# Reordering the first two steps of a windowed-attention and dynamic-convolution kernel on Trainium2

## The chip, the cores and the metric

The kernel runs on one core of one Trainium2 chip. The metric is the device time of one execution in microseconds (us), read as the median of several runs. TensorE is called PE below, its weight loads PEld, VectorE DVE, ScalarE ACT, GpSimd POOL and SyncE SP.

## The reference, cut to what matters

The input is 16 images of 192 channels and 56 x 56 pixels in float32. Layer 0 is a Swin block with shifted 7 x 7 windows and six heads of 32 channels; layer 1 is a depthwise 3 x 3 convolution whose taps are computed from the pooled image.

```python
# layer 0
h = layer_norm(x over channels, norm1_g, norm1_b)      # then roll by (-3, -3), cut into 64 windows of 49
q, k, v = split(win @ qkv_w + qkv_b);  q = q * 32 ** -0.5
attn = softmax(q @ k.T + rel_bias[REL_IDX] + mask)     # mask: 0 or -inf at the rolled edges
x1 = x + unroll((attn @ v) @ proj_w + proj_b)
y = gelu(layer_norm(x1, norm2_g, norm2_b) @ fc1_w + fc1_b) @ fc2_w + fc2_b
x = x1 + y
# layer 1
t = relu(batch_norm(x.mean(height, width) @ w1.T))
taps = (t @ w2.T + b2) * causal_mask                   # 4 of 9 taps survive
out = depthwise_conv3x3(x, taps) + bias
...
```

## The kernel before

An image is done in four steps (`STEPS`) of 784 pixels, sixteen windows each; a step's tokens are two halves of 392 columns. The steps are software-pipelined: while PE does the MLP of one step, the other engines do the softmax and the norms of others. A steady loop over the steps is preceded by a hand-written prologue, which loads and folds the parameters and takes steps 0, 1 and 2 far enough that the loop can start. Its first work on PE is the first layer of the MLP of step 0 (`ph`).

PSUM is used as four pairs of banks. `banks(name, k)` hands out pair `k`; a tile in a pair waits until all readers of the previous tile in that pair are done. So the numbers in the calls decide waits.

```python
def banks(name, k):
    return psum.tile([128, 2, 512], F32, tag=f"pair{k}", name=name)
...
def columns(rows, n, name, k):              # parameter rows to columns: copy, 2 transposes, copy
    nc.vector.tensor_copy(rows[:, DIM:256], rows[:, C0:DIM])
    pt = banks(f"{name}_p", k)[:, 0]
    ...
    nc.vector.tensor_copy(cols.rearrange("p c n -> p (c n)"), pt[:, 0 : 2 * n])
...
def fold_means(dst, n, name, k):            # ones @ weights: fq_m for qkv, ff_m for fc1
...
def shift(dst, raw, lo, n, be):             # one-column products: a norm's bias through a weight
    mm(dst, raw[:, 0, lo : lo + n], be[0], True, False)
    mm(dst, raw[0:64, 1, lo : lo + n], be[1][0:64], False, True)
...
def attention_scores(i, q4, q2, ks):        # sc on PE for 4 pairs of windows; bias added on DVE
    ...
    def top(wp):                            # DVE: max, subtract; ACT: exp
    def share(wp):                          # DVE: sum, reciprocal; POOL: prob = e / sum
```

The prologue's order is the order of recording, and each engine works off its own part of it in that order. Cut to what the argument touches, it runs so:

```python
# --- start
g1, be1, bq, bk, bv = columns(*rows1, 2)
...                                          # statistics of half 0 (st_a)
pm = fold_means(wqkv, 3 * DIM, "fq", 0)
fold_center(wqkv, 3 * DIM, pm)
nc.vector.memset(kbd, 0.0)
g2, be2, f2b, pb, cb = columns(*rows3, 1)
...                                          # 24 one-column products, qkb_p
norm_squares("1_1", 1, 0, nc.scalar, nc.vector)
norm1_scale(0, dvs.pop(0), nc.vector)
...                                          # biases of q and k; statistics st_b
...                                          # 14 loads rel_r and mask_t on SP
dvs.update(norm_spread(keys, dev, tags=("dv1", "yn0"), order=(0, 1)))
...                                          # parameter loads on POOL
# --- step 0
qs[0], outs = attention_qk(0, 1, 0, 3)
pvs, v_rest, v_whole = attention_v(0, (2, 1))
v_rest(); v_whole()
pv = banks("pb_p", 3)                        # 36 one-column products: folded biases of proj and fc1
...
table(AF.Exp)
for f in outs: f()                           # ACT: q and k out of PSUM
for t in vbd: nc.vector.memset(t, 0.0)
...                                          # 24 tiles bias_t on DVE
fold_scale(rawf, g2, wf1, ((0, 0, HID, 1.0),))
...                                          # three adds of pb_p on DVE
attention_v_out(pvs)                         # v out of PSUM, DVE and ACT
top, share = attention_scores(0, *qs.pop(0), (3, 0, 2, 1))
...                                          # transposes of w1 (w1p)
pm = fold_means(wf1, HID, "ff", 0)           # ff_m
qs[1], outs = attention_qk(1, 2, 3, 1)
...                                          # softmax of step 0
prts = [attention_turn(0, wp, (2, 0)[wp % 2]) for wp in range(4)]     # pt
# --- steps 1 and 2
pos = attention_values(0, prts, 1, 2)                                  # po
o = attention_rows(0, pos)
pvs, v_rest, v_whole = attention_v(1, (0, 3)); v_rest(); v_whole()     # pv
...
pp, pair1, p_narrow, p_rest, p_whole = project(0, o, 1, 2)             # pp
p_narrow(); p_rest(); p_whole()
residual(0, pp, pair1)
norm_squares("2_0", 0, 1, nc.scalar)
top, share = attention_scores(1, *qs.pop(1), (0, 3, 2, 1))             # scores of step 1
qs[2], outs = attention_qk(2, 0, 3, 2, between)                        # statistics st_c inside
...                                          # softmax of step 1, square roots, table loads
prts = [attention_turn(1, wp, (0, 2)[wp % 2]) for wp in range(4)]
...
pos = attention_values(1, prts, 3, 0)
...                                          # v of step 2, projection of step 1
pairs = [0, 3, 1, 2]
for i in range(2, NS + 2):                   # the steady loop, first ph
    ...
```

Of the kernel before, what the change touches and what calls it, by code (L numbers as in the profile page):

```python
# [9 lines left out]
AF = mybir.ActivationFunctionType  # L10
ALU = mybir.AluOpType
# [25 lines left out]
def tile_swin_then_dynamic_conv(  # L37
# [102 lines left out]
    def columns(rows, n, name, k):  # L140
# [9 lines left out]
        nc.vector.tensor_copy(cols.rearrange("p c n -> p (c n)"), pt[:, 0 : 2 * n])  # L150
# [97 lines left out]
    def norm_squares(key, i, side, engine, adder=None, tags=None):  # L248
# [12 lines left out]
        for h in range(2):  # L261
            p = slice(h * 64, h * 64 + 64)
            (adder or nc.gpsimd).tensor_tensor(s0[p, h], s0[p, h], s1[p], ALU.add)  # L263
        sqs[key] = s0

# [559 lines left out]


    g1, be1, bq, bk, bv = columns(*rows1, 2)
# [17 lines left out]
    norm_root(part)  # L845
    nc.vector.reciprocal(part, part)
    norm_squares("1_2", 2, 1, nc.gpsimd)
    dvs.update(norm_spread(keys, dev, (nc.sync, nc.scalar)))
    pm = fold_means(wqkv, 3 * DIM, "fq", 0)
    fold_center(wqkv, 3 * DIM, pm)  # L850
    nc.vector.memset(kbd, 0.0)
    g2, be2, f2b, pb, cb = columns(*rows3, 1)
# [11 lines left out]
    norm_squares("1_1", 1, 0, nc.scalar, nc.vector)  # L864
    norm1_scale(0, dvs.pop(0), nc.vector)
# [4 lines left out]
    nc.vector.tensor_scalar(kb, pick, qkb[:, 1:2], None, ALU.mult)  # L870

# [5 lines left out]
    norm_root(part)  # L877
    nc.vector.reciprocal(part, part)


    side = 2 * WS - 1
    for j in range(2):
        for yq in range(WS):
            q = j * 64 + yq * WS
            nc.sync.dma_start(
                rel_r[q : q + WS].rearrange("p (y x) h -> p y (x h)", y=WS),
                bass.AP(
                    rel_bias.tensor,
                    yq * side * HEADS,
                    [[HEADS, WS], [side * HEADS, WS], [1, WS * HEADS]],  # L890
                ),
            )
    nc.sync.dma_start(mask_t, win_mask)
    dvs.update(norm_spread(keys, dev, tags=("dv1", "yn0"), order=(0, 1)))
    images[1] = load_x(1, nc.sync)
    norm_squares("1_3", 3, 0, nc.gpsimd)
    for t in prob:
        nc.gpsimd.memset(t, 0.0)
# [4 lines left out]
    for k, v in enumerate((running_var, running_mean, gamma, beta)):  # L903
        nc.gpsimd.dma_start(bn[:, k], v.rearrange("(o r) -> o r", o=1).broadcast_to([128, RED]))
    w2v = w2.rearrange("(c t) r -> c t r", t=9)[:, 0:NTAP, :]
# [8 lines left out]
    qs[0], outs = attention_qk(0, 1, 0, 3)  # L914
    pvs, v_rest, v_whole = attention_v(0, (2, 1))
    v_rest()
    v_whole()

    pv = banks("pb_p", 3)
# [8 lines left out]
    table(AF.Exp)  # L928
    for f in outs:
        f()  # L930
    for t in vbd:
        nc.vector.memset(t, 0.0)
    rel_hk = rel_r[:, ::-1, :].rearrange("p k h -> p h k")
    for r in range(2):
        for e in range(2):
            for half in range(2):
                for g in range(3):
                    h = 2 * half if g < 2 else 4
                    row_b = g == 1 or (g == 2 and half == 1)
                    cut = mask_t[:, int(r and row_b), e, :].rearrange("p (o k) -> p o k", o=1)  # L940
                    nc.vector.tensor_tensor(
                        bias_t[:, r, e, half].rearrange("p (h k) -> p h k", k=N)[
                            :, 2 * g : 2 * g + 2
                        ],
                        rel_hk[:, h : h + 2],
                        cut.broadcast_to([PW, 2, N]),
                        ALU.add,
                    )
    fold_scale(rawf, g2, wf1, ((0, 0, HID, 1.0),))
    for c in range(2):  # L950
        nc.vector.tensor_tensor(pb[c], pb[c], pv[:, 0, c : c + 1], ALU.add)
# [303 lines left out]
```

## Time and profile before

| | before |
|---|---|
| time, first three runs | 3168.89 us median (3168.42 to 3170.85) |
| span of the profiled execution, clock granted to PE | 3168.7 us, 0.991 |
| from the start to the first `ph` | 125.14 us |
| from the first `ph` to the end of the span | 3043.6 us |
| PE idle before the first `ph` | 26.7 us |

The prediction below shows the main lines of this profile. One more cut of it carries the later argument. The next fence is PE's timeline of the kernel before; its columns are the start, the length, the engine, the line, the operation and its tiles, the count, and in brackets the idle time before it with what ended it.

```profile
94.25 1.48 PE L92 MATMUL pe<-win,wqkv 128*128 128x392 f32 x4
99.84 0.86 PE L519 MATMUL pt<-ident,prob 113*128 113x113 f32 x6 [4.11 <-ACT q L397]
103.56 3.63 PE L519 MATMUL pt<-ident,prob 113*128 113x113 f32 x18 [2.86 <-POOL prob L506]
111.47 5.37 PE L92 MATMUL po<-prt,vbd 128*64 128x49 f32 x96 [4.28 <-ACT kbd L416]
...
125.14 1.56 PE L92 MATMUL ph<-yn,wf 128*128 128x392 f32 x4
```

The first line is the last product of q and k of step 2; it ends at 95.7 us. From there PE has only work that hangs on the softmax of step 1: the turning of its probabilities (`pt`), the weighted values (`po`), v of step 2 and the projection. It stands still before three of these. The table by stretches, cut at 95.7 us (its columns are explained in the prediction), puts numbers to the two parts:

```profile
0.00:95.70 95.70, 80.22 (x604) 49.40 (x604) 62.72 (x159) 37.94 (x68) 39.60 (x62) 0.82 0.38 93
95.70:125.14 29.44, 18.19 (x167) 14.77 (x167) 13.90 (x25) 17.53 (x32) 14.98 (x18) 0.77 0.12 28
```

The second part holds 167 matmuls in 29.4 us, of which PE is busy 18.2 us at a clock of 0.77. Idle time here is idle time of the engine that sets the end, so a microsecond of it that goes, and does not come back elsewhere, is one of the kernel's.

### The profile page before, as it was taken

What the parts mean: (1) busy time and instruction counts of PE and PEld (TensorE: products, weight loads), DVE (VectorE), ACT (ScalarE), POOL (GpSimd) and SP (SyncE); (2) the same over time, 40 slices, a digit from 0 to 9 for tenths busy, and PEclk for the clock granted to TensorE, in tenths of its full rate; (3) what the DMA queues carried; (4) which work ended last, traced back from release to release, by engine and by line L of the source; (5) the groups of instructions that cost most, each with busy time, mean ns of one, the idle gap of its engine ahead of it and who ended that gap; (6) DMA issues with size and microseconds to landing.
All of it is one profiled execution on the core that took longest, in us unless ns stands there. A gap on an engine that the chain in (4) does not pass through costs nothing.

```text
span 3168.7 us, 64205 instructions
## 1 busy us (share of the span) xinstructions
PE 3123.1 (99%) x26162; PEld 1932.8 (61%) x26162; DVE 2126.2 (67%) x3909; ACT 1882.5 (59%) x2990; POOL 975.3 (31%) x882
## 2 busy tenths in 40 slices
PE   8899999999999999999999999999999999999998
PEld 5566566666666666666666666666666666666654
DVE  6645766866766766766767667667667667667664
ACT  3555655656656656556556556556566566566553
POOL 4333233232232332332332332332332332323321
PEclk7999999999999999999999999999999999999999
DMA  4001021111101112011120201211111120111101
GB/s 111 12 21 52 27 63 31 32 57 36 58 27 40 54 32 64 30 52 36 38 57 29 65 26 32 61 32 57 33 43 44 37 62 27 52 39 34 27 27 51
DMA packets 79155, 135.37 MB, mean 43 GB/s; under 512 B 21782, under 2 KB 61468, under 8 KB 76940
## 3 DMA queue, kind: packets, MB, share of 16 engines
q1 hardware_dynamic: 77186, 128.92, 14.0%
q8 instruction: 207, 3.39, 0.5%
q0 software_dynamic: 1168, 1.54, 0.3%
q10 hardware_dynamic: 506, 0.79, 0.1%
q14 instruction: 88, 0.72, 0.1%
HBM read 41.26 MB, written 38.54 MB: 25 GB/s over the span
## 4 chain that ended last, share of the span: by engine, by line
PE 93%; DVE 4%; ACT 3%; issue 0%; DMA 0%; POOL 0%; ACTq 0%; SPq 0%; POOLq 0%; DVEq 0%
PE pf L92 24%; PE ph L92 22%; PE pp L92 8%; PE pv L92 7%; PE po L92 6%; PE pq L92 5%; PE pt L519 5%; PE sc L92 4%; PE st L92 4%; PE pk L92 4%; PE pe L92 4%; DVE vbd L462 1%; DVE x L595 1%; ACT vbd L462 1%; ACT hid L609 0%
## 5 line engine op out<-in xcount | busy, mean ns | idle before, releaser
L92 PE MATMUL ph<-yn,wf 128*128 128x392 f32 (+1 forms) x3072 | 806.2, 499 | 3.8 <-ACT hid L609 3.2
L92 PE MATMUL pf<-hid,wf 128*128 128x392 f32 (+1 forms) x3072 | 802.8, 494 | 3.5 <-ACT hid L609 2.0
L506 POOL TENSOR_TENSOR prob<-e,tot 113x588 f32<-113x588 f32 x256 | 298.2, 1176 | 1189.8 <-DVE tot L505 1168.1
L92 PEld LDWEIGHTS ph<-yn,wf 128*128 128x128 f32 (+1 forms) x3072 | 422.5, 188 | 359.1 <-issue 78.9
L462 ACT COPY vbd<-pv 49x192 f32<-49x192 f32 x512 | 160.5, 314 | 696.2 <-DVE vbd L462 691.6
L92 PEld LDWEIGHTS pf<-hid,wf 128*128 128x128 f32 (+1 forms) x3072 | 386.3, 164 | 303.7 <-issue 120.0
L655 DVE SCALAR_TENSOR_TENSOR x<-pf,cols,x 128x784 f32<-128x784 f32 (+1 forms) x128 | 106.1, 829 | 528.5 <-PE pf L92 485.9
L609 ACT ACTIVATE hid<-ph,f1b 128x784 f32<-128x784 f32 x384 | 337.1, 913 | 100.8 <-PE ph L92 99.4
L263 POOL TENSOR_TENSOR sq<-sq,sq 64x392 f32<-64x392 f32 x252 | 260.4, 1033 | 372.2 <-ACT sq L257 357.9
L718 DVE SCALAR_TENSOR_TENSOR y<-x,wt,y 128x770 f32<-128x770 f32 x282 | 321.1, 1148 | 16.8 <-ACT y L711 8.3
L358 POOL TENSOR_TENSOR yn<-x,dv 128x784 f32<-128x784 f32 x62 | 115.2, 1858 | 534.5 <-DMA dv<-dev 534.5
L92 PEld LDWEIGHTS pv<-wqkv,win 64*128 64x128 f32 (+1 forms) x2048 | 255.7, 189 | 31.5 <-issue 1.2
L92 PE MATMUL pv<-wqkv,win 64*128 64x192 f32 (+1 forms) x2048 | 272.8, 326 | 0.5 <-ACT kbd L416 0.5
L497 DVE TENSOR_TENSOR e<-e,top 113x588 f32<-113x588 f32 x256 | 267.0, 1043 | 8.9
L490 DVE TENSOR_TENSOR e<-sc,bias_t 113x588 f32<-113x588 f32 x256 | 179.4, 763 | 123.8 <-PE sc L92 123.8
L92 PE MATMUL pp<-o,wp 128*128 128x392 f32 (+2 forms) x896 | 251.4, 514 | 0.0
L245 ACT ACT_TABLE_LOAD x193 | 247.6, 1283 | 5.2 <-issue 1.8
L525 ACT COPY prt<-pt 128x678 f32<-128x678 f32 x256 | 179.3, 727 | 116.5 <-PE pt L519 115.1
L500 ACT ACTIVATE e<-e 113x588 f32<-113x588 f32 x256 | 176.8, 691 | 110.0 <-DVE e L497 109.9
L519 PEld LDWEIGHTS pt<-ident,prob 113*128 113x128 f32 x1536 | 166.8, 142 | 72.3 <-issue 39.9
L92 PE MATMUL po<-prt,vbd 128*64 128x49 f32 x6144 | 199.2, 225 | 4.3 <-ACT kbd L416 4.3
L462 DVE COPY vbd<-pv 49x192 f32<-49x192 f32 x512 | 181.2, 354 | 31.9 <-PE pv L92 24.7
(166 smaller groups left out, 3994.8 us busy)
## 6 DMA issues: line engine op xcount, KB each, us to landing
dv<-dev SPq DMA_DIRECT2D x1012, 49.0 KB
x<-in_x_dram SPq DMA_DIRECT2D x15, 1484.0 KB
out_dram<-y SPq DMA_DIRECT2D x48, 392.0 KB
out_dram<-y SPq DMA_DIRECT2D x48, 196.0 KB
x<-in_x_dram SPq DMA_DIRECT2D x16, 392.0 KB
x<-in_x_dram SPq DMA_DIRECT2D x15, 350.0 KB
out_dram<-y SPq DMA_DIRECT2D x16, 308.0 KB
out_dram<-y SPq DMA_DIRECT2D x16, 154.0 KB
```

Of the source, the lines that this page charges most:

```text
L92: nc.tensor.matmul(dst, lhs, rhs, start=start, stop=stop, skip_group_check=True)
L245: nc.scalar.activation(junk, eps_t[0:1], func)
L263: (adder or nc.gpsimd).tensor_tensor(s0[p, h], s0[p, h], s1[p], ALU.add)
L462: copy(dst, src[s * 64 : s * 64 + N, h, :, :, j, :])
L490: nc.vector.tensor_tensor(e, sc[:PW, :, : HEADS * N], rel, ALU.add)
L497: nc.vector.tensor_tensor(ehs[wp], ehs[wp], t.broadcast_to([PW, 2 * HEADS, N]), ALU.subtract)
L500: nc.scalar.activation(es[wp], es[wp], AF.Exp)
L506: nc.gpsimd.tensor_tensor(prob[wp][:PW, :, 0:N], ehs[wp], t.broadcast_to([PW, 2 * HEADS, N]), ALU.mult)
L519: nc.tensor.transpose(pt[:, a, g * PW : (g + 1) * PW], prob[wp][:PW, h : h + 2, :].rearrange("p h k -> p (h k)"), ident[:PW, :PW],)
L525: nc.scalar.copy(prt, pt[:, :, : 3 * PW])
L609: nc.scalar.activation(hid[:, f], phs[f][:, :, :T], AF.Gelu, bias=f1b[:, f : f + 1])
L718: nc.vector.scalar_tensor_tensor(dst, src, wt[:, kc, t : t + 1], dst, ALU.mult, ALU.add)
```

## The change

The intent is to keep PE supplied through the prologue. Four things are moved. At the start, the parameter transpose goes ahead of the mean products, the clearing of `kbd` and `vbd` goes from DVE to POOL (`prob` was cleared there before), and the 14 loads of the relative bias are issued by POOL instead of SP, early, so that a quarter of the bias tiles can be made before q and k. In step 0, the folding of biases (`pb_p`) goes behind the scores, beside the softmax. In step 1, the scores come right behind the weighted values of step 0, ahead of v and the projection. And the means of fc1 (`ff_m`) go behind the projection of step 0. One table load disappears. With the early scores come two things more: the turning and the values of step 1, and q, k and e of step 2, get other bank pairs, and POOL takes the scaling of step 2's window from DVE. The steady loop only begins with its bank pairs in other roles. The diff, cut to its core:

```diff
@@ start
-    def columns(rows, n, name, k):
+    def columns(rows, n, name, k, copy):
...
+    nc.sync.dma_start(mask_t, win_mask)
+    side = 2 * WS - 1
+    for j in range(2):
+        for yq in range(WS):
+            q = j * 64 + yq * WS
+            nc.gpsimd.dma_start(rel_r[...], ...)          # was nc.sync, further down
+    def biases(r, e): ...                                 # 6 of the 24 bias tiles
     norm_root(part)
+    g2, be2, f2b, pb, cb = columns(*rows3, 1, nc.scalar.copy)
     nc.vector.reciprocal(part, part)
     norm_squares("1_2", 2, 1, nc.gpsimd)
+    add = norm_squares("1_1", 1, 0, nc.scalar, False)
...
     fold_center(wqkv, 3 * DIM, pm)
-    nc.vector.memset(kbd, 0.0)
-    g2, be2, f2b, pb, cb = columns(*rows3, 1)
+    add(nc.vector)
...
-    norm_squares("1_1", 1, 0, nc.scalar, nc.vector)
-    norm1_scale(0, dvs.pop(0), nc.vector)
+    biases(0, 0)
...
+    norm1_scale(0, dvs.pop(0), nc.vector)
+    nc.gpsimd.memset(kbd, 0.0)
+    for t in vbd: nc.gpsimd.memset(t, 0.0)
+    for t in prob: nc.gpsimd.memset(t, 0.0)
...
-    dvs.update(norm_spread(keys, dev, tags=("dv1", "yn0"), order=(0, 1)))
+    dvs.update(norm_spread(keys, dev, (nc.sync, nc.gpsimd), tags=("dv1", "yn0"), order=(0, 1)))
@@ step 0
-    pv = banks("pb_p", 3)        # and its 36 products, three adds
...
-    attention_v_out(pvs)
-    top, share = attention_scores(0, *qs.pop(0), (3, 0, 2, 1))
+    fold_scale(rawf, g2, wf1, ((0, 0, HID, 1.0),))
+    attention_v_out(pvs)
+    norm1_scale(1, dvs.pop(0), nc.gpsimd)
...
+    top, share = attention_scores(0, *qs.pop(0), (0, 2, 3, 1))
+    pv = banks("pb_p", 0)        # the 36 products, then the transposes of w1 in the same pair
...
-    pm = fold_means(wf1, HID, "ff", 0)
     qs[1], outs = attention_qk(1, 2, 3, 1)
@@ steps 1 and 2
+    top, share = attention_scores(1, *qs.pop(1), (0, 3, 2, 1))
     pvs, v_rest, v_whole = attention_v(1, (0, 3))
...
+    top(0); top(1); share(0)
+    attention_v_out(pvs)
+    norm1_scale(2, dvs.pop(1), nc.gpsimd)
+    pm = fold_means(wf1, HID, "ff", 0)
+    top(2)
     residual(0, pp, pair1)
     norm_squares("2_0", 0, 1, nc.scalar)
-    top, share = attention_scores(1, *qs.pop(1), (0, 3, 2, 1))
...
-    qs[2], outs = attention_qk(2, 0, 3, 2, between)
+    norm_stats(keys, {0: 3, 1: 0})
+    qs[2], outs = attention_qk(2, 2, 0, 1)
...
+    fold_center(wf1, HID, pm)
-    table(AF.Exp)
...
-    prts = [attention_turn(1, wp, (0, 2)[wp % 2]) for wp in range(4)]
+    prts = [attention_turn(1, wp, (2, 1)[wp % 2]) for wp in range(4)]
...
-    pos = attention_values(1, prts, 3, 0)
-    o = attention_rows(1, pos)
+    o = attention_rows(1, attention_values(1, prts, 2, 1))
...
-    pairs = [0, 3, 1, 2]
+    pairs = [3, 0, 2, 1]
```

## The prediction

> **What bounds the kernel now.** I read the page first: TensorE (PE) is busy for 99% of the span.
>
> ```profile
> PE 3123.1 (99%) x26162; PEld 1932.8 (61%) x26162; DVE 2126.2 (67%) x3909; ACT 1882.5 (59%) x2990; POOL 975.3 (31%) x882
> ...
> PE   8899999999999999999999999999999999999998
> ...
> PEclk7999999999999999999999999999999999999999
> ```
>
> Only the first slice (79 us) has a busy digit of 8 and a clock digit of 7; only the last has another 8. The table by stretches says the same in microseconds (columns: stretch, its length, busy time and count of PE, weight loads, DVE, ACT, POOL, granted clock, DMA share, GB/s):
>
> ```profile
> 0.00:125.00 125.00, 98.27 (x770) 64.14 (x770) 76.62 (x183) 55.47 (x99) 54.58 (x80) 0.81 0.32 77
> 15.00:30.00 15.00, 10.03 (x50) 6.54 (x52) 11.16 (x29) 1.75 (x3) 4.34 (x4) 0.50 0.37 85
> 30.00:45.00 15.00, 14.45 (x85) 9.27 (x73) 11.24 (x27) 9.30 (x14) 13.20 (x19) 0.93 0.28 41
> 45.00:62.00 17.00, 15.95 (x131) 10.97 (x131) 13.16 (x29) 3.90 (x10) 9.13 (x17) 0.52 0.75 213
> 100.00:118.00 18.00, 10.86 (x130) 10.06 (x131) 5.11 (x6) 11.49 (x18) 12.88 (x17) 0.62 0.19 46
> 400.00:3050.00 2650.00, 2646.92 (x22494) 1643.48 (x22490) 1816.22 (x3311) 1613.10 (x2561) 819.49 (x714) 1.00 0.15 42
> ```
>
> From 400 to 3050 us PE idles 3 us in 2650 at full clock. The diff does not touch that loop (it only renames which PSUM bank pair starts in which role), so its 3,043 us, from the first first-layer matmul of the MLP (ph, at 125.14 us in the timeline) to the end, should stay. All there is to win lies before 125 us: 27 us of idle PE (125 less 98.3), and work done at half clock. The waits of PE in that stretch:
>
> ```profile
> PE cols_p L146 <- DVE cols_rows L143: 5.0, 1, 5.0
> PE po L92 <- ACT kbd L416: 4.3, 1, 4.3
> PE cols_p L146 <- DMA cols_rows<-in_L_conv_qkv_b_dram: 4.2, 1, 4.2
> PE pt L519 <- ACT q L397: 4.1, 1, 4.1
> PE pt L519 <- POOL prob L506: 2.9, 1, 2.9
> ```
>
> The first is a parameter transpose that waits behind DVE's 2.0 us clearing of kbd. The others at 96 to 111 us are step 1's softmax, whose probabilities come after step 2's q and k have been issued, when PE has nothing else left. The third, the first load, stays. In the timeline of PE the folding of biases stands alone between the values and the scores of step 0:
>
> ```profile
> 43.01 1.40 PE L92 MATMUL pb_p<-cols,wp 128*128 128x1 f32 x12
> 44.35 5.28 PE L92 MATMUL pb_p<-cols,raw 128*128 128x1 f32 x24
> 49.88 2.23 PE L92 MATMUL sc<-kbd,q 64*64 64x98 f32 x48 [0.25 <-DVE f1b L952]
> ```
>
> Step 0's softmax cannot start until these 6.7 us are over, and DVE's copies of v, queued behind the f1b addition, wait for them too.
>
> **What the Trainium skill says.** "TensorE: Matmul & The Clock Gate", Part 1, What's actually happening: PE runs at half clock after an idle window of about 3.4 us and at full clock after one sustained busy window. The trace agrees in the two values (0.50 and 1.00), but one-column matmuls seem not to count as busy: the clock falls to 0.58 in 45 to 50 us while pb_p keeps PE at 4.75 of 5. "SBUF — State Buffer", Who interferes with whom: a DVE instruction with two SBUF inputs contends with a GpSimd instruction that reads SBUF, not with one that only writes. The trace agrees on the first half (the softmax subtraction, L497, takes 0.77 us alone and 1.31 us beside POOL's prob); so I let the moved memsets cost DVE nothing. "PSUM — Partial Sum Buffer", PSUM bank collisions: two engines are kept off one bank; here ACT's v copies wait for DVE's of the same pair ("ACT vbd L462 <- DVE vbd L462", 6 waits). "DMA: Bandwidth & Descriptors", Issuing engines are not separate DMA queues: several issuing engines save only issue time; here that time is most of it (16 dv issues on SP take 10.0 us, each lands 2.1 us later).
>
> **The change, part by part.**
>
> *Start, to q and k of step 0 (pq at 31.26 us before).* kbd's 2.0 us memset leaves DVE, and the second transpose precedes the mean matmuls fq_m. Its rows come last from a POOL load issued at 8.12 us (5.7 us to landing, about 14); DVE can copy them after L295 at 14.83. So fq_m starts near 15.3, not 13.3, and at half clock takes 3.84 us: four products of 288 columns, 0.96 us each (ff_m's 384 columns take 1.28 each cold, 5.67 us for nearly four on the chain). End 19.2, which puts the centring (1.42) at 19.2 to 20.6 instead of 18.1 to 19.6: a loss of 1.1 us. But qkb_p (4.9 us) follows at 19.2 to 24.1 instead of ending at 27.2. st_b (4.2 us) ends at 28.4 instead of 31.3. DVE after 20.6: square sums beside POOL's squares 1.2 to 1.9, six bias_t tiles 1.4 (5.48 us for 24), q/k biases 1.0, window scaling 3.1; ends at 28.2 to 29.5 because the biases wait for 24.1. pq starts near 29.4: **1.8 us gained**. The rel_r loads, now 14 on POOL at about 0.53 us, end issuing near 17.7; POOL's squares move from 16.0 to about 18, ready near 22.5, needed at 27.
>
> *To the scores of step 0 (last sc at 55.4 before).* q, k, e matmuls and v take 7.0 + 4.4 us: v ends at 40.8. ACT's outputs need 0.9 + 1.9 + 3.5 us and end near 41.2; DVE copies v from 39.7 to 42.7 (2.95 for eight), ACT 42.8 to 44.1 behind it. Last score 44.9: **10.5 us gained in total here**, 6.7 of it pb_p, the rest vbd memsets, table load and 18 bias tiles out of DVE's and ACT's way.
>
> *pb_p after the scores (moved).* It is not removed: 44.9 to 51.6, cold at its end; w1p to 52.0. DVE does its softmax (about 11 us) beside it. q and k of step 1, 6.3 us warm (86 to 96 us less st_c), take about 8.4 because their first products are cold: end 60.4 against 68.6 before (**8 us**; ff_m's 5.7 us, interleaved before, left this place). The inputs are in time: dv of step 1 is issued in halves by SP and POOL from 35.6, landed near 43; POOL scales until 49; probabilities follow POOL's loads at about 53 to 58.
>
> *Rest of the prologue (ph at 125.1 before).* Turning, values and the e outputs take about 7 us from 60.4: e at 67.5, scores of step 1 at 66 to 70 with waits of 1.5 us in all for e and the output copies. v of step 1 4.6 us, projection 3.9: end 78.6. Then ff_m, warm, 2.6 us: its old cold cost was 5.7. Now a wait that was not there: residual (2.2), squares on ACT (1.4), POOL's additions (2.1) come one after the other behind the projection and top(2) on DVE (to 80.0): squares ready at 85.7, st_c done at 86.5, PE idle some 3 us. pe shares its bank pair with ff_m, so it waits for fold_center, behind share(3) on DVE: 88.5, another 1.3 us. q, k, e end at 94.1. The softmax is done by then, so the 4.1 us and 2.9 us waits vanish; what is left is ACT's queue of q, k (2.8), four prt copies (2.8): values start near 97.7, about 2 us idle, and take 3.0 us warm, not 5.4. v of step 2 4.6, projection 3.9: ph at **109.4**.
>
> Sum: 125.1 - 109.4 = 15.7 us. By kind: some 7 us less idle PE, and some 9 us less cold work (sc 2, ff_m 3.1, pt and po of step 1 4.3). I take 1.3 us off for waits that such a hand schedule misses: 14.4, so 3168.9 - 14.4 = **3154.5 us**, or -0.45%.
>
> **The rivals.**
> (1) Waits take the place of those removed: the residual-squares-statistics chain in front of st_c and fold_center in front of pe (5 us above) last longer, because POOL also scales step 2's window from 76 on (5.7 us) and each DVE subtraction beside it costs 1.31, not 0.77. If the idle stretch reaches 4 us, the clock drops as it did after 95.7 to 99.8, and qk, pt and po run cold: 4 to 8 us back, 3159 to 3163. For it: POOL sits on the chain. Against: its work is short there.
> (2) The rel_r loads through POOL land late and hold DVE before the q/k biases: early POOL loads took 5.4 to 6.6 us. Each late us after about 22 costs one; 3 to 4 us, so 3158. Against it: DMA share is only 0.37 after 15 us.
> (3) All hidden: prologue order doesn't matter because PE work is the bound. PE's 27 idle us and 0.81 clock speak against it; it would leave 3169.
> (4) Better than summed: clock stays full through pb_p's end and q/k of step 1 and the waits of 5 us shrink: 20 us, 3149.
>
> **Range and chances.** The whole prize is bounded: even removing all 27 us of idle plus all cold losses (busy time by missing clock: 10.0 x 0.50 + 16.0 x 0.48 + 10.9 x 0.38, about 17) is 44 us, 1.4%, so faster by over 2% (63 us) is out of reach, and a loss of 63 us would need a broken steady loop, which the diff doesn't alter. Sum 15.7, minus 8 for rival 1 and plus 6 for rival 4 give 3147 to 3162; I take 3163, rival 1's end, as the upper limit. Faster 0.01, same 0.985, slower 0.005.
>
> **What would show it.** In the new trace: first ph near 109 to 111; last score of step 0 near 45; pb_p still 6 to 7 us; ff_m about 2.6 us; the 5.0 us wait of cols_p and the pt waits for POOL and q gone; new PE waits before st_c and pe; the span after the first ph unchanged at 3,043 us. Wrong if ph comes after 117 (rivals 1 or 2), or if the loop's length changes.

## The result, and the profile after

The changed kernel takes 3155.55 us (median of 4 runs, 3154.91 to 3155.79) against 3168.65 us (4 runs, 3167.26 to 3170.85) for the kernel before on the same chip. The ratio of times is 0.9958, with a 95% interval of 0.994 to 0.9975. Here and below a ratio is the mean time of one kernel's fast runs over the mean of the other's fast runs of the same rounds, so it is not quite the ratio of the medians quoted. All runs in this document are in the fast state and all results agree with the reference.

The prediction said 3154.5 us. It was right, by 1 us. The page of the profile after, for the three lines shown of before:

```profile
PE 3118.8 (99%) x26162; PEld 1930.8 (61%) x26162; DVE 2119.1 (67%) x3893; ACT 1880.1 (60%) x2989; POOL 998.8 (32%) x919
...
PE   8999999999999999999999999999999999999998
...
PEclk8999999999999999999999999999999999999999
```

Two digits differ: the first slice now has a clock of 8 tenths, and PE's second slice (79 to 158 us) is full. The table by stretches of the profile after, with the same stretches as before:

```profile
0.00:125.00 125.00, 110.08 (x854) 69.73 (x858) 78.29 (x192) 61.23 (x108) 81.64 (x119) 0.88 0.31 78
...
15.00:30.00 15.00, 14.53 (x60) 8.03 (x60) 11.84 (x33) 2.15 (x4) 14.29 (x16) 0.50 0.31 73
30.00:45.00 15.00, 13.70 (x132) 9.45 (x132) 12.84 (x34) 10.82 (x20) 10.45 (x17) 0.90 0.45 133
45.00:62.00 17.00, 17.00 (x93) 13.65 (x94) 11.27 (x22) 5.35 (x7) 16.55 (x25) 0.70 0.61 130
50.00:55.00 5.00, 5.00 (x22) 4.64 (x24) 3.92 (x12) 0.90 (x2) 4.79 (x12) 0.50 0.50 122
...
100.00:118.00 18.00, 18.00 (x158) 12.00 (x155) 10.88 (x33) 10.44 (x21) 8.38 (x8) 1.00 0.02 5
400.00:3050.00 2650.00, 2646.81 (x22515) 1642.16 (x22517) 1819.68 (x3308) 1620.21 (x2571) 812.80 (x709) 1.00 0.15 42
```

PE is busy 14.5 of the 15 us from 15 us on (10.0 before), yet at half clock, and 18.0 of the 18 us from 100 us on (10.9 before), at full clock. From 50 to 55 us PE is busy all the time and its clock is 0.50: that is the end of the one-column products. The loop from 400 to 3050 us is what it was. The waits of PE in the first 130 us of the profile after (who waits for what, total, times, longest):

```profile
PE cols_p L146 <- DMA cols_rows<-in_L_conv_bias_dram: 2.1, 1, 2.1
PE cols_p L146 <- DVE cols_rows L143: 2.1, 1, 2.1
...
PE pe L92 <- DVE wf L177: 1.0, 1, 1.0
PE st_c L92 <- POOL sq L266: 0.9, 2, 0.7
...
PE pq L92 <- DVE win L348: 0.5, 1, 0.5
```

The transposes' wait for DVE fell from 5.0 to 2.1 us, but a wait of 2.1 us for the load of their rows is new; the waits of 4.3, 4.1 and 2.9 us are gone; the two waits that the prediction expected as new are there, with 1.0 and 0.9 us. PE's timeline of the profile after, at the moved parts and at the end of the prologue:

```profile
45.57 1.70 PE L92 MATMUL pb_p<-cols,wp 128*128 128x1 f32 x12
47.20 6.27 PE L92 MATMUL pb_p<-cols,raw 128*128 128x1 f32 x24
...
79.32 3.33 PE L92 MATMUL ff_m<-wf,ones 128*128 128x384 f32 x8
...
93.98 1.48 PE L92 MATMUL pe<-win,wqkv 128*128 128x392 f32 x4
95.30 3.34 PE L525 MATMUL pt<-ident,prob 113*128 113x113 f32 x24
...
99.46 2.77 PE L92 MATMUL po<-prt,vbd 128*64 128x49 f32 x88 [0.45 <-ACT prt L531]
...
110.31 2.14 PE L92 MATMUL ph<-yn,wf 128*128 128x392 f32 x6
```

The turning of step 1's probabilities (`pt`) now follows q and k of step 2 at once, and the first `ph` comes at 110.31 us. Cut where q and k of step 2 end, 95.3 us (the table by stretches again):

```profile
0.00:95.30 95.30, 81.12 (x604) 51.47 (x605) 65.15 (x155) 43.59 (x77) 69.84 (x105) 0.84 0.37 93
95.30:110.31 15.01, 14.27 (x167) 10.82 (x166) 4.63 (x12) 10.91 (x22) 9.62 (x13) 1.00 0.22 56
```

Read against the two stretches of before this is the heart of the case. The counts of matmuls agree, 604 and 167, so the same work is compared. **The first stretch got 0.4 us shorter, the second 14.4 us** (29.4 to 15.0). Where the reordering looks most busy, up to 95 us, it gained next to nothing; what it bought there is that the scores of step 1 end at 71.3 us instead of 87.3. Their softmax is then over when PE needs it: the last of its four subtractions on DVE runs at 84.6 us, before q and k of step 2 are done, where it ran at 99.6 us, 4 us behind them. DVE's timeline, before and after:

```profile
99.56 1.31 DVE L497 TENSOR_TENSOR e<-e,top 113x588 f32<-113x588 f32 x1
```

```profile
84.63 1.43 DVE L503 TENSOR_TENSOR e<-e,top 113x588 f32<-113x588 f32 x1
```

Of the 14.4 us, 10.5 are idle time of PE (29.44 less 18.19, against 15.01 less 14.27), and the other 3.9 are shorter busy time: `pt`, `po` and v now run at a clock of 1.00.

One of the three waits that are gone does not hang on the softmax. In the kernel before, `po` of step 1 takes bank pair 3, which `pe` of step 2 holds (`attention_qk(2, 0, 3, 2)`, e being the second number, and `attention_values(1, prts, 3, 0)`). ACT copies `pe` out behind the four `prt` copies, and `po` starts at 111.47 us, when the last of these copies is done. In the changed kernel `pe` is in pair 0 and `po` takes pairs 2 and 1; `po` starts at 98.57 us, though ACT is done with `pe` only at 102.9. ACT's last copy of `pe`, before and after:

```profile
110.23 1.18 ACT L416 ACTIVATE kbd<-pe,qkb 32x392 f32<-32x392 f32 x2
```

```profile
101.68 1.18 ACT L422 ACTIVATE kbd<-pe,qkb 32x392 f32<-32x392 f32 x2
```

So the wait of 4.3 us goes with the new pair numbers. Had `po` still waited for `pe`, it would have started some 4 us later (an estimate from 98.57 and 102.9). No run changes the pairs alone, so the early softmax is shown as the cause of at most the other two waits.

The part from the first `ph` to the end is the same in all profiles: the time of a profiled run less its first `ph` is 3045.4 us for the kernel before, 3044.6 for the changed one, and 3044.2 to 3045.8 over all thirteen profiled kernels of this document. So differences below of more than those 1.6 us arise before the first `ph`, and one can look for their cause in the prologue alone.

### The profile page after: what moved, and what is told of

Its sections match the earlier page's. It is cut to its first block, busy times and chain, and to the rows that moved or that the text cites. A ratio compares the mean times of both kernels' runs of the same rounds, so it can differ in the third digit from the quotient of the medians.

```text
span 3153.1 us, 64205 instructions
## 1 busy us (share of the span) xinstructions
PE 3118.8 (99%) x26162; PEld 1930.8 (61%) x26162; DVE 2119.1 (67%) x3893; ACT 1880.1 (60%) x2989; POOL 998.8 (32%) x919
## 4 chain that ended last, share of the span: by engine, by line
PE 92%; DVE 4%; ACT 2%; DMA 1%; issue 1%; POOL 0%; ACTq 0%; SPq 0%; POOLq 0%; DVEq 0%
PE pf L92 24%; PE ph L92 22%; PE pp L92 8%; PE pv L92 7%; PE po L92 6%; PE pq L92 5%; PE pt L525 5%; PE sc L92 4%; PE st L92 4%; PE pk L92 4%; PE pe L92 4%; DVE vbd L468 1%; DVE x L601 1%; ACT hid L615 0%; ACT y L717 0%
## 5 line engine op out<-in xcount | busy, mean ns | idle before, releaser
L266 POOL TENSOR_TENSOR sq<-sq,sq 64x392 f32<-64x392 f32 x252 | 260.3, 1033 | 349.9 <-ACT sq L257 335.6
L245 ACT ACT_TABLE_LOAD x192 | 246.3, 1283 | 5.2 <-issue 1.8
L92 PEld LDWEIGHTS po<-prt,vbd 128*64 128x64 f32 x6144 | 188.9, 138 | 9.7 <-ACT prt L531 0.6
```

The source lines that it names most:

```text
L92: nc.tensor.matmul(dst, lhs, rhs, start=start, stop=stop, skip_group_check=True)
L245: nc.scalar.activation(junk, eps_t[0:1], func)
L266: adder.tensor_tensor(s0[p, h], s0[p, h], s1[p], ALU.add)
```

## The experiments

What had to be told apart: which half of the change earns the time, and whether the halves add; whether moving the folding matters, as the prediction's 6.7 us said; what the start is bound by, now that it has the new loads on POOL; and whether one-column products that hold the clock down are worth placing elsewhere. The theory was the prediction's: waits removed behind step 1's softmax and cold work made warm, with the first half needed to bring the scores forward. The rivals were that one half does it alone, that the moved folding was hidden anyway, and that the start is bound by the loads. The table gives all runs; the three groups ran on three chips, each with the kernel before in its own rounds. "End of q, k" is the end of q and k of step 2 in the profile, "last stretch" the time from there to the first `ph`. The ends in this table are the modelled ends of the last product, which can overlap the next one by some 0.2 us; so it has 95.5 us for the changed kernel where the cut above was put at 95.3.

| run | median us (range, 5 runs) | before us | ratio (95%) | end of q, k | last stretch | first `ph` |
|---|---|---|---|---|---|---|
| before, first profile | | | | 95.7 | 29.4 | 125.1 |
| changed, first profile | | | | 95.5 | 14.8 | 110.3 |
| undo_second | 3168.28 (3165.97 to 3169.57) | 3168.55 | 0.9998 (0.9984 to 1.0011) | 94.8 | 27.4 | 122.2 |
| only_second | 3161.19 (3159.71 to 3161.86) | 3168.55 | 0.9974 (0.9961 to 0.9986) | 100.5 | 15.4 | 115.9 |
| undo_fold_move | 3163.65 (3163.01 to 3164.18) | 3168.55 | 0.9983 (0.997 to 0.9995) | 104.2 | 14.8 | 119.1 |
| no_fold | 3153.57 (3153.0 to 3154.52) | 3168.55 | 0.9951 (0.9939 to 0.9964) | 95.1 | 14.8 | 109.9 |
| after_again | 3155.87 (3152.73 to 3157.21) | 3169.45 | 0.9957 (0.9944 to 0.9969) | 98.0 | 15.0 | 113.0 |
| rel_late | 3153.18 (3151.71 to 3154.07) | 3169.45 | 0.9948 (0.9935 to 0.9962) | 93.2 | 15.0 | 108.3 |
| fold_spread | 3155.12 (3153.88 to 3156.45) | 3169.45 | 0.9956 (0.9944 to 0.9969) | 95.3 | 15.4 | 110.7 |
| both | 3150.87 (3150.03 to 3152.58) | 3169.45 | 0.9944 (0.9931 to 0.9956) | 90.5 | 15.3 | 105.8 |
| only_first | 3168.57 (3168.07 to 3170.6) | 3169.68 | 1.0 (0.9986 to 1.0013) | 94.1 | 28.8 | 123.0 |
| warm | 3157.37 (3156.49 to 3158.44) | 3169.68 | 0.9962 (0.9949 to 0.9974) | 98.0 | 15.3 | 113.3 |
| both_warm | 3150.07 (3148.23 to 3151.19) | 3169.68 | 0.9938 (0.9925 to 0.995) | 90.0 | 15.4 | 105.5 |

The ratios' intervals reach some 4 us to either side. Five runs of a kernel spread over 1.2 to 4.5 us, and a profile is one of these runs, so two profiles of the same kernel (110.3 and 113.0) differ as much as some of the kernels do.

### undo_second: the first half of the change alone

The changed kernel up to the turning of step 0, then the order of before, with `ff_m` behind the projection of step 0.

```diff
     o = attention_rows(0, pos)
-    top, share = attention_scores(1, *qs.pop(1), (0, 3, 2, 1))   # scores of step 1 early
     pvs, v_rest, v_whole = attention_v(1, (0, 3))
...
     p_whole()
+    pm = fold_means(wf1, HID, "ff", 0)
     residual(0, pp, pair1)
+    fold_center(wf1, HID, pm)
     norm_squares("2_0", 0, 1, nc.scalar)
+    top, share = attention_scores(1, *qs.pop(1), (0, 3, 2, 1))
...
-    pairs = [3, 0, 2, 1]
+    pairs = [0, 3, 1, 2]
```

> The changed kernel with everything after step 0's output rows put back into the old order (values, projection and residual of step 0 before the scores of step 1; step 1's softmax behind q and k of step 2; window scaling of step 2 on DVE), the mean products of fc1 kept behind the projection. Theory 'order' (most of the 13 us comes from step 1's softmax being started before other PE work): the 4.1, 2.9 and 4.3 us waits of PE near the transposes and weighted values come back with half clock behind them; the first MLP matmul lands 8 to 11 us later, 3164 to 3167 us. Rival 'relief' (the gain comes from the memsets, tiles and copies taken off DVE and from the folding move in the first half, which this keeps): 3156 to 3158 us.

It measured 3168.28 us against 3168.55: no gain that can be seen, where 3164 to 3167 us were expected. In its waits the 4.3 us of `po` and the 3.3 and 2.9 us of `pt` are back (the first of them with the old bank pairs, which the edit brings back too), and its last stretch is 27.4 us. A new wait came with the edit: the scores of step 1 stand 2.0 us for the centring behind `ff_m`. This leaves a doubt: the placing of `ff_m` costs this kernel 3.33 us of products and 2.0 us of waiting. The run only_first was made to answer it.

### only_first: the same with ff_m where it cost before

```diff
# against undo_second
     nc.vector.tensor_copy(w1t, ...)
+    pm = fold_means(wf1, HID, "ff", 0)         # right behind q and k of step 1
     top(3); share(2); share(3)
+    fold_center(wf1, HID, pm)
...
-    pm = fold_means(wf1, HID, "ff", 0)
     residual(0, pp, pair1)
-    fold_center(wf1, HID, pm)
```

> The changed kernel's first half with the old second half, as undo_second, but fc1's mean products right behind q and k of step 1 and their centring behind step 0's softmax, so that the old order meets no new wait (undo_second's trace has a 2.0 us wait of PE for the centring that I had built in). If the halves simply add (only_second gained 7.4 us of 13.1): 3162.5 to 3164 us. If part of the gain exists only with both halves, because the new order hides the 3.3 us mean products in the wait for the residual and the old one has no place for them: 3165 to 3167 us.

It measured 3168.57 us against 3169.68, ratio 1.0, slower than expected. Its waits of PE:

```profile
PE po L92 <- ACT kbd L422: 4.3, 1, 4.3
PE pt L525 <- ACT q L403: 4.1, 1, 4.1
...
PE pt L525 <- POOL prob L512: 2.4, 1, 2.4
...
PE pt L525 <- DVE wf L177: 1.3, 1, 1.3
```

The first three lines are the three waits of before, nearly unchanged, though its first stretch was done at 94.1 us, 1.6 us before that of the kernel before. The last is `pt` standing behind the centring of fc1. So `ff_m` lies on PE's path in either placing, and the first half alone leaves the last stretch at 28.8 us. Whatever it gains early, it waits for step 1's softmax at the end.

### only_second: the second half of the change alone

The kernel before up to the turning of step 0, with `ff_m` and the folding in their old places, then the changed order.

```diff
# against before
+    top, share = attention_scores(1, *qs.pop(1), (0, 3, 2, 1))
     pvs, v_rest, v_whole = attention_v(1, (0, 3))
...
-    top, share = attention_scores(1, *qs.pop(1), (0, 3, 2, 1))
...
-    qs[2], outs = attention_qk(2, 0, 3, 2, between)
+    norm_stats(keys, {0: 3, 1: 0})
+    qs[2], outs = attention_qk(2, 2, 0, 1)
...
-    table(AF.Exp)
...
-    pairs = [0, 3, 1, 2]
+    pairs = [3, 0, 2, 1]
```

> The kernel before with only the second half of the change (from step 0's output rows on), first half untouched. Theory 'order': gains 8 to 11 us on the kernel before, 3158 to 3161 us, more than the first half alone (the run undo_second). Rival 'relief': 3166 to 3168 us. If the halves add, the gains of undo_second and of this run sum to about 13 us.

It measured 3161.19 us, 7.4 us under the kernel before: more than half of the gain of 13.1 us, from this half alone. Its last stretch is 15.4 us, 14.0 us shorter than before. But its first stretch ends at 100.5 us, 4.8 us later than before. The price of bringing the scores forward is there: PE now waits before the statistics of step 0's residual for ACT's copies of v, for the residual itself and for POOL's sums (1.1, 1.0 and 0.9 us before `st_c`), and from the end of the projection to the first product of q for step 2 takes 8.3 us (85.8 to 94.1). In the changed kernel the same way takes 8.3 us (79.5 to 87.8), with the 3.33 us of `ff_m` in it. **There the products of `ff_m` fill a wait.** Their place is only nearly free: `pe` waits 1.0 us for the centring behind them, a wait that only_second does not have, and from the end of the projection to the end of q and k of step 2 the changed kernel takes 16.0 us and only_second 14.7. In only_second it stands cold on the path ahead of q and k of step 1, for 5.7 us. Taking it from there belongs to the first half, giving it a nearly free place to the second: this is where the two interlock. With both, the first stretch ends at 95.5 us in one profile and 98.0 in the other, so 2.5 to 5.0 us of the 4.8 come back.

The sum of the two halves alone is 7.4 + 0.3 to 1.1 us; together they gain 13.1. That the two need each other is what the traces show of `ff_m`; that the surplus is as much as 5 us is not settled, with intervals of 4 us on each ratio.

### undo_fold_move: the folding back in front of the scores

```diff
# against the changed kernel
     for f in outs: f()
+    pv = banks("pb_p", 0)       # 36 products, transposes of w1
     fold_scale(rawf, g2, wf1, ((0, 0, HID, 1.0),))
+    ...                         # three adds, copy of w1t
     attention_v_out(pvs)
...
-    top, share = attention_scores(0, *qs.pop(0), (0, 2, 3, 1))
-    pv = banks("pb_p", 0)       # 36 products, transposes of w1
+    top, share = attention_scores(0, *qs.pop(0), (2, 0, 3, 1))
```

> The changed kernel with the bias folding pb_p (36 records, 7.9 us in its trace) put back ahead of the scores of step 0, and DVE's additions ahead of its v copies. My account: the products cost PE the same either way, so what the move buys is the softmax of step 0 running beside them: scores 8 us later, q and k of step 1 at the same time, softmax ends about 8 us later than 57.5 and holds the transposes from 61.4 to about 66: 4 to 5 us slower than the changed kernel, 3159.5 to 3161 us. Rival: all 7.9 us are lost, 3163 us; or the transposes were bound by q and k anyway, under 1 us.

It measured 3163.65 us, some 8 us slower than the changed kernel (3155.55 and 3155.87 in the other groups): more than expected, and near the 3163 us of the recorded rival. PE's timeline of this kernel says where:

```profile
50.89 0.52 PE L955 MATMUL pb_p<-ident,w1n 48*128 48x48 f32 x2 [2.09 <-DMA w1n<-in_L_conv_w_dram]
...
68.85 4.34 PE L525 MATMUL pt<-ident,prob 113*128 113x113 f32 x24 [4.39 <-ACT q L403]
```

The transposes of w1 wait 2.1 us for their load, which is a fault of this edit and not of the old order. The scores run cold behind that (2.23, 1.25 and 1.25 us; 1.23, 0.73 and 0.73 in the changed kernel). They end at 57.5 us, so step 0's softmax ends late and `pt` waits 4.4 us for ACT, which has the exponentials ahead of q in its queue; then `pt` itself is cold, 4.34 us (2.72 in the changed kernel). Moving one-column products behind the scores therefore matters, by up to 8 us, of which 2 belong to the edit.

### no_fold: the folding left out

The 36 products and their three adds are taken out. The result stays right only because the biases that they fold are zero in these inputs. This is a measurement and not a version to use.

```diff
     pv = banks("pb_p", 0)
-    mm(pv[:, 0, 0:1], ...)      # 12 products for proj, 24 for fc1
...
-    nc.vector.tensor_tensor(f1b, f1b, pv[:, 1, :NFC], ALU.add)      # and two for pb
```

> The changed kernel without the folding products and their three additions (outputs stay right only because norm1_b, qkv_b and norm2_b are zero here): measures what pb_p costs where the change put it. My account: q and k of step 1 could start at 45.6 instead of 53.5, but POOL's scaling of step 1's window ends at 51.3, so the transposes come only some 2 to 3 us earlier, with PE idle about 5 us and perhaps a cold clock: 3152.5 to 3154 us. Rival: the 7.9 us lie wholly on the path, 3147.5 us. If neither PE nor POOL but the softmax on DVE holds them, under 1 us gained.

It measured 3153.57 us, 2 us under the changed kernel's median, which the intervals of the two ratios do not separate. Eight microseconds of PE work gone, and at most some two of them gained. The trace shows why. Its start was slower in the profile (the last score at 48.3 us, 45.6 in the changed kernel), and from there to the first `ph` it needs 61.6 us where the changed kernel needs 64.7: so 3.0 us were won. That stretch varies little where the folding stands as in the changed kernel (64.7 and 64.9 us in its two profiles, 64.9 in rel_late, 65.2 in warm). Most of the rest is a wait that the folding had covered: the transposes of w1 now stand 3.4 us for their load, which POOL issues. The folding is therefore not free where the changed kernel puts it; taking it away merely uncovers another wait. A version with w1 loaded earlier as well was not run.

### after_again: the changed kernel once more

> The changed kernel itself, on the same chip and in the same rounds as the next three, to compare them with and to see whether its first 30 us vary: in its first profile q and k of step 0 start at 29.05 us, but at 30.4 to 31.3 in three experiments with the same start. If my reading is right (loads of rel_r through POOL land at chance times and push POOL's squares and DVE's additions), this profile shows a start between 29 and 31.5 us; the time is 3154 to 3157 us.

No edit; it was run as the base for its group. It measured 3155.87 us against 3169.45, a gain of 13.6 us. Its profile is the less lucky one: q and k of step 0 start at 30.54 us, where the first profile had 29.05.

### rel_late: relative-bias loads behind the first normalisation loads, on SP

```diff
-    nc.sync.dma_start(mask_t, win_mask)
-    ...                          # 14 loads rel_r on POOL
...
     dvs.update(norm_spread(keys, dev, (nc.sync, nc.scalar)))
+    ...                          # 14 loads rel_r on SP, then mask_t (in a buffer of its own)
...
-    biases(0, 0)                 # ahead of the biases of q and k
...
-    biases(0, 1)
     nc.vector.reciprocal(part, part)
     ...
-    biases(1, 0); biases(1, 1)
+    biases(0, 0); biases(0, 1)   # all steps but the last of an image
...
     share(3)
+    biases(1, 0); biases(1, 1)
```

> The changed kernel with the rel_r and mask loads back on SP behind the first dv, and the bias tiles behind the reciprocal of steps 1 and 2 (those of the last window row behind step 0's softmax), so that POOL's squares and DVE's additions at 19 to 26 us run undisturbed. Theory (the start's gain that I predicted, 1.8 us, is mostly lost to POOL's 14 loads and to DVE waiting[...]): L266 on DVE returns from 2.6-3.8 us to 1.2, q and k of step 0 start at st_b's end, 28.5 to 29 us, and the kernel gains 1 to 2 us: 3153.5 to 3155 us. Rival (the start is bound by the chain fq_m, centring, folding and st_b at half clock): no gain, 3155 to 3156 us.

It measured 3153.18 us, 2.7 us less than after_again in the same rounds; the ranges of the two overlap, so the size of the gain is not settled. The mechanism is in two engines' timelines. In the changed kernel POOL's queue (loads, then its squares):

```profile
14.00 0.59 POOL L838 DMA_DIRECT2D rel_r<-in_L_conv_rel_bias_dram  x1 [0.99 <-DMA rel_r<-in_L_conv_rel_bias_dram]
...
18.43 1.51 POOL L259 TENSOR_TENSOR sq<-x 128x784 f32<-128x784 f32 x1
...
20.81 2.30 POOL L266 TENSOR_TENSOR sq<-sq,sq 64x392 f32<-64x392 f32 x2
```

The first line is a load that waited for an earlier one to land; the second is the squares, at 18.43 us, and the third POOL's sums of them. In rel_late the squares start at 15.66 us. DVE has its own sums of squares (L266) right after the centring; in the changed kernel they run beside POOL's work (here beside its sums, in after_again beside its squares too):

```profile
20.96 2.57 DVE L266 TENSOR_TENSOR sq<-sq,sq 64x392 f32<-64x392 f32 x2
```

and in rel_late they do not:

```profile
21.22 1.15 DVE L266 TENSOR_TENSOR sq<-sq,sq 64x392 f32<-64x392 f32 x2
```

The same two additions take 2.57 us and 1.15 us (4.07 in after_again, 3.45 in warm). So the bias tiles, the q and k biases and the window scaling behind them on DVE come later, and PE's first q waits for the window: 0.5 us in the first profile, 2.7 in after_again, 0.3 in rel_late, where it starts at 28.63 us. Three things were changed at once here (the issuing engine, the place of the tiles, the mask's buffer); which of them is worth what was not told apart.

### fold_spread: 24 of the folding products moved on

The fc1 part of the folding goes into the wait before the statistics of step 0's residual, where `ff_m` is in the changed kernel; `ff_m` goes behind q and k of step 1.

```diff
-    for f in range(NFC): shift(pv[:, 1, f : f + 1], rawf, f * 128, 128, be2)
     qs[1], outs = attention_qk(1, 2, 3, 1)
...
+    pm = fold_means(wf1, HID, "ff", 0)      # and the transposes of w1
...
+    fold_center(wf1, HID, pm)
...
-    pm = fold_means(wf1, HID, "ff", 0)
+    pv = banks("f1_p", 0)
+    for f in range(NFC): shift(pv[:, 1, f : f + 1], rawf, f * 128, 128, be2)
```

> The changed kernel with the 24 fc1 folding records moved from before q and k of step 1 into the wait before st_c's squares, fc1's mean products with their centring moved from there into the wait for step 0's softmax, and POOL's parameter loads put behind its scaling and first probabilities. If, as the run no_fold suggests, the folding lies on the path but POOL's scaling (51.3) holds q and k as well: q and k of step 1 start near 49, transposes near 58.8 instead of 61.4, and the 1.0 us wait of pe for the centring goes: 3 to 4 us faster than the changed kernel, 3151.5 to 3153 us. Rival: a new wait (softmax on DVE, w1n's load, or a cold clock) eats it: 3154 to 3156 us.

It measured 3155.12 us, 0.75 us under after_again, which is within the spread: nothing shown. q and k of step 1 are done 5.1 us sooner than in the changed kernel (56.5 against 61.6), but that is given back: `ff_m` now stands in the path, `pt` waits 1.4 us for the copy of w1, and q and k of step 2 end at 95.3 us, as in the changed kernel.

### both: rel_late and fold_spread together

> rel_late and fold_spread together. If their gains add (they act in different stretches): 3150 to 3152 us. If the earlier start of step 0 is swallowed by POOL's scaling of step 1 or by the softmax: as fold_spread, 3152 to 3153 us.

The edit is the sum of the two above. It measured 3150.87 us, 5.0 us less than after_again in the same rounds, and no run of it was as slow as the fastest of after_again. Its first `ph` is at 105.76 us. It beats both kernels, the one before by 18.6 us of medians. Its median is 2.3 us under that of rel_late, with overlapping ranges, though fold_spread alone showed nothing: with the start not waiting for loads, the earlier q and k of step 1 (done at 51.8 us) seem to be of use. The trace shows what it still pays: behind the 24 one-column products in the wait the clock is 0.50 (79 to 84 us), and the statistics there take 2.84 and 2.46 us. The products alone do not decide this: in fold_spread (80 to 90 us) and both_warm (75 to 85 us) they stand in the same place and the clock stays at 1.00.

### warm: keeping PE busy at the start

The start is cold: 0.50 from 15 to 30 us. Five unread products between the first statistics and the transposes close the gap in which the clock falls.

```diff
     norm_stats(keys, {0: 0})
+    wm = banks("warm", 0)
+    for h in range(5):
+        mm(wm[:, 0, :T], ones, flat_of(0)[0][:, h % 2], True, True)
```

> The changed kernel with five matmuls whose result nobody reads (about 0.8 us each) in PE's idle time between the first statistics and the parameter transposes, to keep the clock full: tests what the half clock at 15 to 30 us costs. Theory from after_again (there fq_m ended 0.8 us earlier, yet q and k started at 30.5 because DVE was held by POOL): the start is bound by POOL's loads and squares, so under 1 us gained, 3155 to 3156 us. Rival (cold fq_m, 5.1 us, bounds the start): 2 us gained, 3153 to 3154 us.

It measured 3157.37 us, above both expectations: no gain (1.5 us more than after_again, other rounds). The products did what they should: `fq_m` takes 2.79 us (5.10 in the first profile), `qkb_p` 3.16 (4.99). Yet PE's timeline says:

```profile
30.70 1.14 PE L92 MATMUL pq<-win,wqkv 64*128 64x392 f32 x2 [4.07 <-DVE win L348]
```

q of step 0 starts at 30.70 us, after 4.1 us of waiting for the window. The time saved on PE is spent waiting for DVE, whose sums take 3.45 us beside POOL and whose bias tiles wait 1.5 us for the last `rel_r` to land. The start is bound by that chain, not by PE's clock.

### both_warm: the same five products in the best version

> The run both with the same five unread matmuls. There POOL no longer holds DVE, so here the cold clock should count: fq_m 3.3 instead of 5.1 us, q and k of step 0 at 26 to 27 us instead of 28.7, and 1.5 to 2.5 us gained on both: 3148.5 to 3149.5 us. Rival: the first dv's landing or POOL's squares hold step 0's window, under 0.7 us gained: 3150.3 to 3151 us.

With the loads out of the way the five products bring q of step 0 forward from 28.71 to 25.39 us. By the first `ph` this has shrunk to 0.3 us (105.48 against 105.76). Most of it goes where the clock falls again: the first twelve products of q, k and e take 4.2 us instead of 2.6 in step 0 (25.39 to 29.56; 28.71 to 31.33) and 3.6 instead of 2.4 in step 1. The time, 3150.07 us with a ratio of 0.9938 against 0.9944, is the lowest of all and lies between the two expectations, but the intervals overlap, so no gain over both is shown.

## Why the prediction was right

The number came out within 1 us. Step by step it was less exact, and two errors of 5 to 6 us had opposite signs: that the sum came so close is partly luck.

- **The bound.** The claim that everything happens before the first `ph` and that the loop stays held in all runs. The first `ph` was predicted at 109.4 us and came at 110.31, in the second profile at 112.99. The text took 1.3 us off its sum of 15.7 for missed waits; the medians gained 13.1, so about twice that was right.
- **Start.** q and k of step 0 were predicted for 29.4 us; they came at 29.05 and 30.54. Rival 2 was real in another form. It expected late loads to hold DVE; what happened is mostly that POOL's issues hold POOL's squares and sums, beside which DVE's sums take longer (predicted at 1.2 to 1.9 us, measured 2.57 and 4.07). `fq_m` was sized by columns at 3.84 us and took 5.10 and 4.12.
- **Scores and folding.** The last score was predicted at 44.9 us and came at 45.6; the folding at 6.7 us, and it took 1.70 + 6.27 us, with the clock at 0.50 from 50 to 55 us. POOL's scaling of step 1's window was to end at 49 us and ended at 51.3. The folding was also told as running beside the softmax, and no_fold shows that some of it is on the path. The step that the old place costs was right, as undo_fold_move shows.
- **The new waits.** The text put about 5 us of waiting before `st_c` and `pe` and 2 us before the values. They measured 0.9, 1.0 and 0.45 us. Rival 1, that the clock would fall there, did not happen: it stayed at 1.00 from 85 to 100 us. The chain of residual, squares and sums itself was told well: its last sums were to be ready at 85.7 us and were at 87.0. What was too small is PE's own work ahead of them. The projection ended at 79.5 us (78.6 told), `ff_m` took 3.33 us (2.6), and the part of the statistics that does not need the last sums kept PE busy until 85.3 us.
- **By kind.** "Some 7 us less idle PE, and some 9 us less cold work" was the mis-sized split. Before the first `ph` PE idles 26.7 us before (125.14 less 98.41 busy) and 14.9 after (110.31 less 95.39): 11.8 us less idle, and only 3.0 less busy. The idle term was too small by the 4.7 us of waits just named. The cold term was too large: the scores gained 2.0 as told, `ff_m` 2.3 instead of 3.1, `pt` and `po` 3.3 instead of 4.3, and `fq_m` (1.5) and `pb_p` (1.3) lost what had not been counted; some 1.8 us are spread over smaller groups.
- **Readings that were off.** The text put the 4.3 us before `po` down to step 1's softmax; it was the copies of `pe` in the bank pair that `po` takes, as shown above. It came out right because the changed kernel gives `po` other pairs. "Each lands 2.1 us later" is the median of POOL's eight dv issues; the view gives no landing for SP's. And ACT's copies of v, which wait for DVE's, read the other bank of the pair (`attention_v_out` gives `pv[:, 0]` to DVE and `pv[:, 1]` to ACT), so they do not wait for one bank; what for is not shown.
- **kbd's clearing on POOL** was said to cost DVE nothing. The small DVE operation behind the q and k biases (kb) took 0.87 us beside POOL's clearings, and 1.52 in the second profile; in the kernel before, without them, it took 0.21. But it took 0.21 in warm as well, where POOL was clearing too, so the overlap alone does not explain it. DVE's sums of squares were not held by the clearing: 1.15 us in rel_late beside that of `kbd`, and 1.15 in the kernel before.

What the prediction missed as an insight is the place of the gain. It told 10.5 us of gain at the scores of step 0 and 8 us at q and k of step 1. Much of that was a loan: `pb_p` and `ff_m`, 6.7 and 5.7 us before, were only put off, and once they are paid (8.0 and 3.3 us) the end of q and k of step 2 stands where it was. The text's own milestones hold this (94.1 against 95.7 us), but it did not say it. The 14.4 us are in the last stretch, and undo_second and only_first, with 27.4 and 28.8 us there, show that early gains do not reach the end without the second half.

**What stays open:** the size of what the halves gain only together, what of the second half is worth how much (the early scores, the bank pairs, the scaling on POOL, the table load), the parts of rel_late by themselves, and whether the five products add anything to both. Why two profiles of the changed kernel start q and k of step 0 1.5 us apart is also not known; the POOL issues' waits differ (1.0 and 0.5 us in one, 1.8 and 0.4 in the other), and in the second POOL stood 1.6 us more for the load of `wp` before it issued them, but no run controls this.

## What to carry to other kernels

Follow a gain to the end of the stretch it is in: cut both timelines at the same piece of work (equal counts of matmuls) and compare the lengths, since time won early is often only waited away later. A cost in the path can be made nearly free by placing it in a wait that exists anyway, as `ff_m` was between a projection and the statistics that hang on it, but whether that wait exists depends on the other half of the schedule. And before warming or shortening the bounding engine's start, look at what it waits for next: here it was a transfer issued by an engine that had other work to do.

## What the Trainium skill lacked or had wrong

- "TensorE: Matmul & The Clock Gate", Part 1, What's actually happening: the page says that sustained activity raises the clock. It does not say that behind products with one column the clock can fall though the record has PE busy all the time: from 50 to 55 us of the changed kernel PE is busy 5.00 of 5 us and its clock is 0.50, and in the run both it is 0.50 from 79 to 84 us, behind the 24 products of fc1's folding. It need not fall: in fold_spread and both_warm it stayed at 1.00 behind the same 24. What decides is not known.
- "ScalarE: Activation LUTs", What ACT_TABLE_LOAD costs: the page gives about 1283 ns for the load and about 1380 ns of drain on top. The load agrees (192 loads of 1283 ns mean in the changed kernel). The trace shows no such drain around it: there the activation ahead of the load at 88.90 us ends at 88.88, and the one behind it starts at 90.19, 0.01 us after the load.
- No page that was read tells that an engine's issue of a load can stand until an earlier load, of the same tile or of another, has landed. In the changed kernel issues of `rel_r` on POOL waited 1.0 and 0.5 us for earlier ones and 0.35 us for a load of `raw`, in warm 1.6 and 0.7, and SP stood 3.7 us for the landing of `mask_t` before the first normalisation loads.
